# Moving the read-back of attention sums within the rounds of a macaron transformer block

## The chip, the cores and the metric

The kernel runs on one core of a Trainium2 chip. A core has five engines that run side by side: TensorE (matrix products, PE in the profile), VectorE (DVE), ScalarE (ACT), GpSimd (POOL) and SyncE (SP), which here does nothing but issue transfers (DMAs). Each engine works through its own instructions in order. The metric is the time of one launch on the device in microseconds (us); lower is better.

## The reference

One layer in the macaron form: half a feed-forward block, attention, half a feed-forward block, each on the layer-normed input and each added to it. The input is 2 sequences of 1024 tokens, 256 channels.

```python
x = x + 0.5 * ffn(layernorm(x))
x = x + attn(layernorm(x))      # q, k, v with bias, rotary turn, causal
x = x + 0.5 * ffn(layernorm(x))

# attn: 32 query heads of 8 channels, 8 key/value heads, each shared by 4 query heads
scores = einsum('bhqd,bhkd->bhqk', q, k_rep) / sqrt(8)
attn   = softmax(where(kpos > qpos, -inf, scores))
out    = einsum('bhqk,bhkd->bhqd', attn, v_rep)
return out.reshape(B, T, C) @ Wo + bo

# ffn: keep the 2 largest of each 4 hidden values
h = silu(x @ w_gate) * (x @ w_up)
return sparsify_2to4(h) @ w_down
```

## The kernel before

**Units and rounds.** Attention is cut into 16 units, one for each sequence `b` and key/value head `g`; a unit holds 4 query heads, taken as two pairs. Each unit has two passes. Pass 1 (`pass1`, L584 and the masks at L599) computes scores and takes their row maxima on VectorE (L613). Pass 2 (`pass2`, L669) computes the transposed scores with the maximum already subtracted, ScalarE takes the exponential (L679), and `weighted` (L706) multiplies by the values. A value tile has a column of ones beside the values, so the sum of the exponentials comes out of the same product.

Round `n` works on three units at once: pass 2 of unit n−1 (`prev`), pass 1 of unit n (`cur`), and the preparation of unit n+1 (`nxt`). The order of these pieces is written out by hand in the text `order`: `p1` and `p2` are pieces of the passes, `av k` multiplies piece `k` by the values, `neg1` and `shift` turn maxima into rows, and `prep` transposes the next unit (L529, `hT`), copies it (`stage`) and sends it to its place by 14 transfers (L543 zeros, L550 `kT`, L557 `qT`). The rounds from 1 on run under a hand-given schedule for TensorE and GpSimd; VectorE, ScalarE and SyncE are put in order by the scheduler of the language, which may place an instruction earlier or later than the text has it.

**Rows of maxima.** `shift` transposes the maxima (L640), copies them to `mrow` (L648), and sends four rows of 2x512 values, one for each head, into `qT` (L651). The first two heads (0 and 1) use strips of pair 0, the last two (2 and 3) those of pair 1. The rows of half 1 are first needed by `p2 3 1`, which is pass 2 on pair 1.

**PSUM.** Score tiles (`s`), the transposes `hT` and the output product share three buffers of two banks each, so TensorE is never more than three such tiles ahead of VectorE and ScalarE.

**From the products to the output.** When a unit has finished half of its queries (`av 2` for the first half, `av 9` for the second), `oT` is copied out of PSUM (L716) and stored to a buffer `avs` in DRAM (L717). After the last unit of a sequence, `output(b, blk)` brings the whole half together. It is a generator with stages: first it reads the sums and the products back from `avs`, eight transfers (L730 `sums`, L731 `heads`); then comes a reciprocal on VectorE (L733), its store to DRAM (L735 `recs`) and four transfers that spread it (L737 `heads<-recs`); then the multiplication (L742) and the product with `wo` (L753), which for the first sequence are made much later, in the last part of the attention. So for the first sequence the stages up to L737 happen inside the rounds of the second sequence:

- first half: `av 2` of round 8 makes the generator and takes its first stage at once; the second stage is called at `av 5` of round 9;
- second half: `av 9` is placed early in the order, and this one is made by round 9, which takes the first stage at once; the second stage is called at `av 5` of round 10.

The lists are `outs` (all generators), and `divisions` (those whose second stage is still to come).

Of the kernel before, what the change touches and what calls it, by code (L numbers as in the profile page):

```python
# [35 lines left out]
def macaron_kernel(  # L36
# [349 lines left out]
    def attention(actx, beside_first, beside_last, outs):  # L386
# [419 lines left out]
        units = [(b, g) for b in range(B) for g in range(NKV)]  # L806
        made = {}
        beside = []
        divisions = []

        def step(op, prev, cur, nxt):
            kind, *arg = op
            if kind == "p1" and cur is not None:
                cur.pass1(*steps1[arg[0]], arg[1:] or (0, 1))
            elif kind == "p2" and prev is not None:
                es = prev.pass2(*steps2[arg[0]], arg[1:] or (0, 1))
                made.setdefault(arg[0], (prev, {}))[1].update(es)
            elif kind == "av" and arg[0] in made:
                unit, es = made.pop(arg[0])
                qh, kbs = steps2[arg[0]]  # L820
                last = arg[0] in (2, 9)
                unit.weighted(qh, kbs, es, last)
                if last and unit.g == NKV - 1:
                    outs.append(output(unit.b, qh))
                    next(outs[-1])
                    if unit.b < B - 1:
                        divisions.append(outs[-1])
            elif kind == "neg1" and prev is not None:
                prev.negated(1)
            elif kind == "shift":  # L830
                unit = prev if arg[0] == 1 else cur
                if unit is not None:
                    unit.shift(arg[0])
            elif kind == "prep" and nxt is not None:
                nxt.prepare()
# [18 lines left out]
        def a_step():  # L854
            while beside and next(beside[0], beside) is beside:
                beside.pop(0)

        def round_(n, prev, cur):
            nxt = Unit(*units[n + 1]) if n + 1 < len(units) else None
            if n == 1:  # L860
                beside.append(second)
            if nxt is not None and nxt.b == 1:
                for _ in second:
                    pass
            firsts = 0
            for i, op in enumerate(ops):
                step(op, prev, cur, nxt)
                if i == first and cur is not None:
                    cur.negated(0)
                if n == 0 and i == first:  # L870

                    nc.scalar.activation(warm, cur.maxima[0][:, 0, 6:7], AF.Exp, scale=0.0)
                if n == 0 and op[0] == "p1":
                    firsts += 1
                    if firsts <= 12:
                        for _ in range(2 * (firsts % 2)):
                            next(beside_first, None)
                if n > 0:
                    for _ in range(2 if op in PAIRS else op[0] in ("av", "prep")):
                        a_step()  # L880
                if n > NKV and op == ("av", 5) and divisions:
                    next(divisions.pop(0))
            return cur, nxt

        engines = {mybir.EngineType.PE, mybir.EngineType.Pool}
        with tc.tile_pool(name="att_round0", bufs=2, side="right") as late["2"]:
            with tc.manual_schedule(engines=engines):
                prev, cur = round_(0, prev, cur)
                for _ in beside_first:
                    pass  # L890
# [6 lines left out]
        with tc.manual_schedule(engines=engines):  # L897
            for n in range(1, len(units)):
                prev, cur = round_(n, prev, cur)
        rctx.close()  # L900
        yield
        with tc.manual_schedule(engines=engines | {mybir.EngineType.DVE}):
            for op in parsed(last_order):
                if op[0] == "b":
                    next(beside_last, None)
                else:
                    step(op, prev, None, None)
            for _ in beside_last:
                pass

    with ExitStack() as fctx:
        actx = ExitStack()
        gens, outs = {}, []
# [23 lines left out]
        with last_units:  # L937
            first = FFN(0, False, f0 := ExitStack(), wd_sb, last_pool)
            att = attention(actx, first.down_slowly(NTB - 1), second_starts(), outs)
            with f0:  # L940
                first.run(
                    """
                    l0 l0 l0 l1 g0 l1 g0 l2 g0 g0 l2 g0 m l1 g0 g0 l2 m g0 m g1 m g1 m g1 m
                    g1 g1 m g1 d0 m a d0 l3 a p g1 p g1 m g2 m p g2 m g2 m p p p g2 p d1 m m
                    g2 m d1 a a l3 g2 p g2 l3 p g2 m p g3 p p m g3 p p m g3 g3 g3 m g3 m g3
                    m g3 p m m m d2 d2 a a
                    """,
                    {"p": att},
                )
            next(att)  # L950
# [71 lines left out]
```

## Time and profile before

| | us |
|---|---|
| median of 3 runs | 820.93 |
| lowest, highest | 820.42, 822.25 |
| profiled execution | 824.67 |
| its span, first to last instruction | 822.9 |
| TensorE busy | 786.1 |
| VectorE busy | 654.7 |
| ScalarE busy | 426.9 |
| GpSimd busy | 236.2 |

The profiled execution is one run of its own, with a time somewhat above the median. Its mean granted TensorE clock is 0.99 of full speed. Timelines give start and length of each instruction from the start of the span; an idle time before an instruction stands in brackets with what ended it. `SPq` is SyncE's queue: a line there is the issue of a transfer, not its landing. In shapes such as `64*128 64x512` the first is the stationary operand. A round lasts about 25.7 us when nothing disturbs it; round 10 begins at about 460 us of the span.

### The profile page before, as it was taken

The page shows a single profiled execution, that of the slowest core. Times are in us where ns is not written, and L with a number is a line of the kernel's source. Part 1 is how long each engine was busy: PE and PEld are TensorE (multiplying, and loading weights), DVE is VectorE, ACT ScalarE, POOL GpSimd, SP SyncE. Part 2 cuts the span into 40 slices and gives each one's busy share as a digit, 9 for nine tenths or more (in the row PEclk, how much of TensorE's full clock was granted, in tenths as well). Part 3 has the DMA queues.
Part 4 walks back from the last instruction along what each step waited for, and adds up shares of the span by engine and source line. Part 5 has one row for each costly group of instructions (what it writes and reads, how often), then busy time and mean ns, then how long its engine had stood idle before and what let it go on. Part 6 is the DMA issues. An engine that isn't in the chain of part 4 may idle for free.

```text
span 822.9 us, 13949 instructions
## 1 busy us (share of the span) xinstructions
PE 786.1 (96%) x5344; PEld 426.4 (52%) x5344; DVE 654.7 (80%) x871; ACT 426.9 (52%) x531; POOL 236.2 (29%) x443
## 2 busy tenths in 40 slices
PE   5999999998899999999999999999999999999998
PEld 2447574476544444454444444444445445657466
DVE  4797999898768796888888788888885479788692
ACT  1331313211677776877787687878877423122210
POOL 3000294821265465464222322233223100000000
PEclk9999999999999999999999899999999999999999
DMA  8100000022213222311333323322202200000001
GB/s 276 31 0 2 0 2 0 0 41 41 33 27 64 44 46 50 67 31 44 66 68 70 93 65 68 56 44 51 57 28 92 74 1 16 1 26 1 11 16 51
DMA packets 31010, 36.03 MB, mean 44 GB/s; under 512 B 12896, under 2 KB 20960, under 8 KB 30944
## 3 DMA queue, kind: packets, MB, share of 16 engines
q1 hardware_dynamic: 29118, 31.85, 17.2%
q10 hardware_dynamic: 1826, 3.29, 1.2%
q8 instruction: 42, 0.69, 0.4%
q14 instruction: 24, 0.20, 0.1%
HBM read 10.75 MB, written 10.75 MB: 26 GB/s over the span
## 4 chain that ended last, share of the span: by engine, by line
PE 71%; DVE 22%; ACT 4%; issue 1%; POOL 1%; DMA 0%; DVEq 0%; ACTq 0%
PE gu L252 20%; PE av L706 16%; PE s L584 9%; PE s L669 9%; PE o L307 9%; DVE maxima L613 8%; ACT e L679 3%; DVE h L292 2%; PE pr L474 2%; PE oo L753 2%; DVE h L262 1%; DVE sg L261 1%; DVE b L275 1%; PE s L599 1%; PE hT L529 1%
## 5 line engine op out<-in xcount | busy, mean ns | idle before, releaser
L613 DVE TENSOR_REDUCE maxima<-s 128x2 f32<-128x1024 f32 (+2 forms) x288 | 343.2, 1220 | 67.2 <-PE s L584 44.3
L679 ACT ACTIVATE e<-s 128x1024 f32<-128x1024 f32 x288 | 287.4, 1023 | 83.4 <-PE s L669 75.1
L706 PE MATMUL av<-e,vaug 128*32 128x512 f32 (+3 forms) x1536 | 158.5, 501 | 0.0
L685 POOL TENSOR_SCALAR_AFFINE_SELECT e<-e 128x256 f32<-128x256 f32 (+1 forms) x224 | 98.3, 451 | 201.5 <-ACT e L679 201.0
L584 PE MATMUL s<-kT,qT 64*128 64x512 f32 (+3 forms) x768 | 133.3, 386 | 14.6 <-ACT e L679 11.7
L669 PE MATMUL s<-qT,kT 64*128 64x512 f32 (+3 forms) x768 | 134.7, 395 | 3.1 <-DVE maxima L613 2.2
L252 PE MATMUL gu<-xnT,wg_sb 128*128 128x512 f32 x256 | 122.3, 600 | 0.7 <-ACT xnT L206 0.7
L252 PE MATMUL gu<-xnT,wu_sb 128*128 128x512 f32 x256 | 120.4, 593 | 0.0
L307 PE MATMUL o<-wd_sb,h 128*128 128x256 f32 x512 | 116.6, 386 | 0.9 <-DVE x L340 0.8
L584 PEld LDWEIGHTS s<-kT,qT 64*128 64x128 f32 x768 | 67.9, 187 | 82.7 <-ACT e L679 37.2
L307 PEld LDWEIGHTS o<-wd_sb,h 128*128 128x128 f32 x512 | 98.1, 193 | 18.5 <-issue 3.7
L669 PEld LDWEIGHTS s<-qT,kT 64*128 64x128 f32 x768 | 67.5, 186 | 62.1 <-DVE maxima L613 32.9
L260 ACT ACTIVATE sg<-gu 128x512 f32<-128x512 f32 x64 | 38.0, 593 | 113.6 <-PE gu L252 113.6
L263 ACT ACTIVATE a<-h 128x512 f32<-128x512 f32 x64 | 40.3, 630 | 104.9 <-DVE h L262 104.8
L252 PEld LDWEIGHTS gu<-xnT,wu_sb 128*128 128x128 f32 x256 | 48.9, 191 | 61.8 <-issue 61.8
L261 DVE TENSOR_TENSOR sg<-sg,gu 128x512 f32<-128x512 f32 x64 | 43.6, 681 | 46.1 <-ACT sg L260 46.0
L252 PEld LDWEIGHTS gu<-xnT,wg_sb 128*128 128x128 f32 x256 | 48.6, 192 | 54.6 <-issue 50.0
L181 POOL TENSOR_TENSOR rstd<-ve,neg_half 128x4 f32<-128x4 f32 x12 | 12.2, 1015 | 194.1 <-DVE ve L179 192.3
L706 PEld LDWEIGHTS av<-e,vaug 128*32 128x32 f32 x1536 | 34.1, 109 | 50.2 <-issue 38.8
L262 DVE TENSOR_TENSOR h<-sg,gu 128x512 f32<-128x512 f32 x64 | 43.9, 687 | 2.2
L599 PE MATMUL s<-half_id,half_mask 64*128 64x64 bf16 (+1 forms) x768 | 43.8, 205 | 0.0
L292 DVE SCALAR_TENSOR_TENSOR h<-w,h 128x512 f32<-128x512 bf16 x64 | 43.7, 743 | 0.0
(80 smaller groups left out, 562.4 us busy)
## 6 DMA issues: line engine op xcount, KB each, us to landing
avs<-oT SPq DMA_DIRECT2D x32, 256.0 KB
qT<-stage SPq DMA_DIRECT2D x124, 64.0 KB
kT<-stage SPq DMA_DIRECT2D x124, 32.0 KB
qT<-mrow SPq DMA_DIRECT2D x128, 4.0 KB
heads<-avs SPq DMA_DIRECT2D x16, 128.0 KB
out<-x SPq DMA_DIRECT2D x7, 256.0 KB
wu_sb<-in_wu SPq DMA_DIRECT2D x2, 512.0 KB
wg_sb<-in_wg ACTq DMA_DIRECT2D x2, 512.0 KB
```

Of the source, the lines that this page charges most:

```text
L252: nc.tensor.matmul(out=gu[:, i, :], lhsT=w_sb[:, kc, gb, j, :], rhs=self.xnT[tb][:, kc, :], start=(kc == 0), stop=(kc == 1),)
L261: nc.vector.tensor_tensor(sg, sg, gu[:, 0, :], ALU.mult)
L262: nc.vector.tensor_tensor(h[:, j, :], sg, gu[:, 1, :], ALU.mult)
L292: nc.vector.scalar_tensor_tensor(h[:, j, :], w[:, j, :], at, h[:, j, :], op, ALU.mult)
L307: nc.tensor.matmul(out=o[:, i, :], lhsT=self.hms[tb][k // 4][:, k % 4, bass.ts(2 * t2 + i, P)], rhs=self.wd_sb[:, k // 4, k % 4, :], start ...
L584: nc.tensor.matmul(out=to[:, i, s, bass.ds(col, n)], lhsT=self.qT[strip, pair, bass.ts(qt, P)].bitcast(FR), rhs=self.kT[strip, bass.ds(kc ...
L599: nc.tensor.matmul(out=last.rearrange("p (t n) -> p t n", n=P)[:, :, bass.ts(h, STRIP)], lhsT=half_mask[strip, h, :], rhs=half_id[strip, N ...
L613: ins = nc.vector.tensor_reduce(dst, src, AX.X, ALU.max, negate=True)
L669: nc.tensor.matmul(out=to[:, i, s, bass.ds(col, n)], lhsT=self.kT[strip, bass.ts(kb, P)].bitcast(FR), rhs=self.qT[strip, pair, bass.ds(q0, ...
L679: nc.scalar.activation(e, to, AF.Exp, scale=SCALE)
L685: nc.gpsimd.affine_select(out=first, in_=first, pattern=[[0, 2], [0, len(pairs)], [1, P]], compare_op=ALU.is_ge, fill=0.0, base=0, channel ...
L706: nc.tensor.matmul(out=self.av[32 * i : 32 * i + 32, TB - n : TB], lhsT=vaugs[self.b][:, kb, bass.ds(self.g * VW, 32)], rhs=es[i][:, bass. ...
```

## The change

The first stage of `output` (the eight read-backs of L730 and L731) is no longer taken at once for the first sequence. The generator goes on a list `stored`, and at `av 4` of the same round all of that list take their first stage and pass to `divisions`. For the first half this is `av 4` of round 8, for the second half `av 4` of round 9. For the second sequence nothing changes. The second stages are still called at `av 5` of rounds 9 and 10.

```diff
         beside = []
+        stored = []
         divisions = []
...
                 if last and unit.g == NKV - 1:
                     outs.append(output(unit.b, qh))
-                    next(outs[-1])
                     if unit.b < B - 1:
-                        divisions.append(outs[-1])
+                        stored.append(outs[-1])
+                    else:
+                        next(outs[-1])
...
                 if n > NKV and op == ("av", 5) and divisions:
                     next(divisions.pop(0))
+                if op == ("av", 4):
+                    for out_ in stored:
+                        next(out_)
+                    divisions.extend(stored)
+                    stored.clear()
```

In the built program the order on TensorE, ScalarE and GpSimd is the same as before. On SyncE and VectorE, around the end of round 9 and the start of round 10, it becomes (with the number of instructions; `mrow_1` are the rows of unit (1,1)):

```
SyncE before                          SyncE after
avs<-oT  (unit 7, second half)        avs<-oT  (unit 7, second half)
qT<-mrow_1 x3                         qT<-mrow_1 x4
sums, heads <-avs x8                  avs<-oT  (unit 8, first half)
qT<-mrow_1                            sums, heads <-avs x8
avs<-oT  (unit 8, first half)         recs<-sums (first half)
recs<-sums (first half)               qT<-mrow_1 x3      (next half)
qT<-zeros                             heads<-recs x4
heads<-recs x4                        qT<-mrow_1
qT<-mrow_1 x4      (next half)        qT<-zeros
kT, qT <-stage ...                    kT, qT <-stage ...

VectorE before                        VectorE after
maxima p1 1                           maxima p1 1
reciprocal (second half)              maxima p1 5 0
maxima p1 5 0                         maxima p1 0 0
maxima p1 0 0                         maxima p1 9 0
maxima p1 9 0                         reciprocal (second half)
maxima p1 0 1                         maxima p1 0 1
```

## Prediction

> **What bounds the kernel now.** I read the page first, then the timeline of the round in which the change acts, engine by engine, then busy time by stretch with the granted clock, and last the order of instructions on each engine in the two built programs.
>
> From the page, busy time and span:
>
> ```profile
> span 822.9 us, 13949 instructions
> PE 786.1 (96%) x5344; PEld 426.4 (52%) x5344; DVE 654.7 (80%) x871; ACT 426.9 (52%) x531; POOL 236.2 (29%) x443
> ```
>
> TensorE is occupied for 96% of the span, so only what leaves TensorE idle, or slows its clock, can cost or bring time. SyncE (the queue that issues nearly all DMAs) counts only where a matmul waits for a transfer.
>
> The change acts in rounds 8 to 10 of the attention, about 425 to 495 us. The timeline of SyncE's queue at the end of round 9 and the start of round 10:
>
> ```profile
> 451.58 0.51 SPq L717 DMA_DIRECT2D avs<-oT  x1
> 452.19 1.97 SPq L651 DMA_DIRECT2D qT<-mrow  x3
> 455.88 0.31 SPq L730 DMA_DIRECT2D sums<-avs  x1
> ...
> 459.57 0.59 SPq L651 DMA_DIRECT2D qT<-mrow  x1
> ...
> 460.69 0.41 SPq L735 DMA_DIRECT2D recs<-sums  x1
> ...
> 462.58 1.75 SPq L737 DMA_DIRECT2D heads<-recs  x4
> 464.42 2.48 SPq L651 DMA_DIRECT2D qT<-mrow  x4
> ```
>
> The read of the second half's sums stands behind its own store (451.58) and waits for it until 455.88; the fourth row of maxima for unit (1,1), ready long before, is queued behind it and leaves at 459.57. The waits of this queue put that wait at 1.6 us. Does TensorE pay for it? The timeline of TensorE where those rows are used, and the same place one round later:
>
> ```profile
> 460.74 0.50 PE L669 MATMUL s<-qT,kT 64*128 64x512 f32 x2
> 461.44 0.55 PE L669 MATMUL s<-qT,kT 64*128 64x512 f32 x2
> ...
> 464.94 0.93 PE L529 MATMUL hT<-ident_r,part 128*80 128x128 f32 x8 [0.80 <-DVE maxima L613]
> ...
> 493.45 0.79 PE L529 MATMUL hT<-ident_r,part 128*80 128x128 f32 x8 [0.20 <-DVE maxima L613]
> ...
> 497.83 0.50 PE L669 MATMUL s<-qT,kT 64*128 64x512 f32 x2
> ```
>
> The pair that needs the late row starts at 461.44, 0.70 after the pair before it. One round later the same two start at 489.86 and 490.56, also 0.70 apart. So the late row arrives just in time, and the wait that the change removes is worth nothing, 0.07 us at most (0.55 against 0.48 for the pair). The row at 464.94 shows what does cost: the transposes for the next unit wait 0.80 for VectorE instead of 0.20. VectorE's timeline says why:
>
> ```profile
> 461.72 1.23 DVE L613 TENSOR_REDUCE maxima<-s 128x4 f32<-128x1024 f32 x1 [0.27 <-PE s L599]
> 462.86 0.94 DVE L733 RECIPROCAL sums<-sums 128x128 f32<-128x128 f32 x1
> ```
>
> The reciprocal of the second half's sums stands in the row of maxima for which TensorE waits. And behind it, in the busy times by stretch (columns: stretch, its length, busy PE, PEld, DVE, ACT, POOL, granted clock, DMA share, GB/s):
>
> ```profile
> 305.00:308.42 3.42, 2.74 (x24) 1.36 (x22) 3.42 (x5) 2.23 (x3) 2.32 (x5) 1.00 0.51 78
> 308.42:311.83 3.41, 3.41 (x24) 1.41 (x26) 2.74 (x3) 2.45 (x3) 3.41 (x4) 0.50 0.52 82
> 441.54:444.95 3.41, 2.71 (x24) 0.90 (x16) 3.41 (x5) 2.67 (x3) 0.71 (x2) 1.00 0.47 71
> 462.02:465.43 3.41, 2.18 (x25) 1.61 (x25) 3.41 (x4) 2.81 (x4) 1.40 (x5) 1.00 0.31 86
> 465.43:468.84 3.41, 3.41 (x27) 1.86 (x25) 1.80 (x2) 2.43 (x3) 0.61 (x2) 0.50 0.11 20
> 468.84:472.26 3.42, 3.42 (x28) 1.35 (x24) 2.43 (x3) 1.16 (x2) 1.10 (x3) 0.50 0.53 78
> 464.94:493.45 28.51, 27.25 (x257) 13.17 (x257) 21.82 (x22) 20.39 (x23) 7.03 (x18) 0.88 0.30 64
> 493.45:519.10 25.65, 24.58 (x256) 12.11 (x256) 21.82 (x22) 20.73 (x24) 7.05 (x18) 1.00 0.27 56
> ```
>
> After a stretch with 1.23 us of TensorE idle (3.41 less 2.18) the clock is halved for 6.8 us, and the round from 464.94 lasts 28.51 instead of 25.65: 2.86 us lost. The same happened once before, at 308, after 0.68 idle. But 0.70 idle (441.54) did not do it.
>
> **The change, part by part.** In the built programs all engines but SyncE and VectorE keep their order.
>
> *First half (round 8).* Its eight transfers are called five steps later in the text but stand at the same place of SyncE's queue, and its reciprocal at the same place of VectorE's. Worth 0.
>
> *Second half, reads.* Eight transfers of about 0.46 each (455.88 to 459.47) go behind the fourth row of maxima and the next unit's store. They still start when their own store has landed, 455.88, and end at about 459.5, when the queue has nothing urgent: the next row is ready only at 463.9 (the copy at 463.32 lasts 0.57). The fourth row leaves 5 us earlier; by the 0.70 above, worth 0 to −0.07. I take 0.
>
> *Second half, reciprocal.* It moves three maxima later, behind that of p1 9 0. Before, it made the transposes late: 461.37 (exponential) to 464.94 is 3.57, one round later 490.48 to 493.45 is 2.97: it costs 0.60 there. In its new place VectorE has 0.25 of slack ahead of the next maximum (496.26 in the clean round), so 0.94 − 0.25 = 0.7 remain. The reciprocal of the first half, which stands two maxima further on in round 9, agrees: from the transposes to the products of av 1 (437.99 to 447.32) takes 9.33 against 8.62 in the clean round (493.45 to 502.07), 0.71.
>
> *Second half, what is pushed back in the queue.* recs<-sums of the first half (0.41) stays ahead of round 10's rows of maxima, in time when the queue is empty. But heads<-recs (four transfers, 1.75) now stand between the third and the fourth row, and qT<-zeros (0.68) behind the fourth. This adds a wait. Clean-round times less 29.11 (490.48 − 461.37) give round 10: rows start at 463.92, three take 1.97, heads<-recs 1.75 and 0.15 between, so the fourth starts at 467.8, not at 465.85. Its landing is shown by no row. Bounds: not before its issue ends (0.6, so no wait at all); recs<-sums needs 1.89 from issue to the transfer that waits for it (460.69 to 462.58), and the row issued at 459.57 was used at 461.44, 1.87. I take 1.9: landed at 469.7. The matmul that needs it (p2 3 1, second strip) would run at 497.83 − 29.11 = 468.72: 1.0 us late, between 0 and 1.0. Everything on TensorE queues behind it, and ScalarE's exponential (498.39) starts as its pair ends, so a delay here reaches the path whole. It runs beside the 0.7 of the reciprocal, for TensorE waits once for the later of the two: 1.0 together, 1.7 if they added.
> The transfers of the next unit start 2.2 us later (zeros 0.7, rows 1.5) and end at about 480.7 instead of 478.5; the rows of shift 0 behind them end at 484 instead of 481.8 and are first used at 489.86 (the place of 460.74 one round on). The cover is 5.9 us, the landing 1.9; nothing.
>
> *Sum for round 10:* −0.6 + 1.0 = +0.4 us (ends −0.6 and +1.1), without the clock.
>
> *The clock.* Here a rule and the trace disagree. The trace halves the clock after 1.23 us and after 0.68 us of idle in pieces within 3.41 us. The Trainium skill, "TensorE: Matmul & The Clock Gate", section "HAM oscillation — how this bites in real kernels", puts the abstract rule as no idle gaps over about 3.4 us. By the rule neither kernel loses clock here, and the sum is +0.4 whatever moves. By the row, the idle that leaves (0.6 at 464) was worth 2.86 us in this execution, and the idle that comes (up to 1.0 at 469) can cost as much. I follow the row.
> The sum against the profiled execution: 824.67 (span 822.9, 1.8 around it) + 0.4 is 825.1 with a half-speed stretch, and 822.2 without. It lies 3.7 above the median of 820.93. Taking off 2.86 and at most 1.7 (half of the 3.41 at 308) leaves 820.1, about the lowest run shown (820.42). So the runs behind the median mostly lack these stretches, and the change can't take from the median what is not in it: 820.93 + 0.4 = 821.3.
>
> **The rivals.** What a measurement of this kernel tells from no change is about 0.2%, 1.6 us.
> *A, forecast, 0.48: nothing to be seen.* 821.3, its own range 820.3 to 822.4. For it: the removed wait had no one waiting.
> *B, 0.34: slower.* The late fourth row and the reciprocal now fall within 2 us of each other, just ahead of 0.30 of idle that every round has (499.47 in the clean one). With 1.0 that is 1.3 us of idle within 3 us, as much as the 1.23 that halved the clock, and closer together, so that in most executions one stretch holds it. Price: one half-speed stretch 1.7, two 2.86, and 0.4: 823.0 to 824.2, say 823.5. It decides if idle in one stretch passes a point between 0.7 and 1.2. Against it: before had as much idle and its runs mostly show no loss.
> *C, 0.18: faster.* The runs of before do hold the half-speed stretch of round 10, the profiler's own cost hides it in my comparison, and moving the reciprocal ends it: 820.93 − 2.86 + 0.2 = 818.3. Against it: the lowest run would then have to hold it too.
> *That the change does not do what it says* holds for its first half, which does not move; it is part of A.
>
> **How the numbers follow.** Within 0.2% is 819.3 to 822.6. A gives 0.44 to no change, 0.03 to slower, 0.01 to faster; B 0.33 slower, 0.01 same; C 0.16 faster, 0.02 same. Faster 0.17, same 0.47, slower 0.36. The range from 818.4 to 823.7 takes in A, most of C and most of B; about 0.1 is left on each side.
>
> **What would show it.** In the profile after: the fourth row of maxima at about 454.2 and its pair still at 461.44; transposes of round 10 with 0.20 of idle; heads<-recs between the third and fourth row, and the first pair of p2 3 1 up to 1.0 late (right for the new wait; if it is on time, rows land faster than 1.9). Wrong would be A if most executions show the clock halved at 469 to 476 (B), or if the runs drop by over 1.6 us with no half-speed stretch in round 10 (C). A round 10 longer than 27 us at full clock would mean that the two delays add.

## The result, and the profile after

| us | before | changed |
|---|---|---|
| median of 16 runs each, same chip | 820.70 | 822.95 |
| lowest, highest | 820.09, 822.87 | 821.74, 826.08 |
| profiled execution (its span) | 824.67 (822.9) | 822.53 (820.8) |

The ratio is 1.0027, with a 95% interval of 1.0016 to 1.0038: slower by about a quarter of a per cent, 2.25 us between the medians. This ratio, here and below, compares all runs of both kernels; it is not the quotient of the medians, and since the times fall into several humps the two can differ. The two profiled executions stand the other way round, because that of before happened to hold a double half-speed stretch. So neither can be read without the granted clock.

The page of the changed kernel, span and busy times:

```profile
span 820.8 us, 13948 instructions
PE 782.9 (95%) x5344; PEld 425.6 (52%) x5344; DVE 655.2 (80%) x871; ACT 426.7 (52%) x531; POOL 236.2 (29%) x443
```

Nothing in these totals tells of a slower kernel. The timeline of SyncE's queue at the end of round 9 and the start of round 10 (start, length, issue):

```profile
450.85 2.63 SPq L651 DMA_DIRECT2D qT<-mrow  x4
...
458.03 0.37 SPq L735 DMA_DIRECT2D recs<-sums  x1
...
462.59 1.90 SPq L651 DMA_DIRECT2D qT<-mrow  x3
464.58 2.74 SPq L737 DMA_DIRECT2D heads<-recs  x4
467.36 0.59 SPq L651 DMA_DIRECT2D qT<-mrow  x1
467.99 0.67 SPq L543 DMA_DIRECT2D qT<-zeros  x1
```

The first line has all four rows of maxima together: the row that waited for a store now leaves at once. The cost stands lower down: `heads<-recs` lies between the third row and the fourth, and takes 2.74, where it took 1.75 before. TensorE in the same stretch:

```profile
459.41 0.50 PE L669 MATMUL s<-qT,kT 64*128 64x512 f32 x2
460.11 0.48 PE L669 MATMUL s<-qT,kT 64*128 64x512 f32 x2
...
463.01 0.79 PE L529 MATMUL hT<-ident_r,part 128*80 128x128 f32 x8 [0.21 <-DVE maxima L613]
...
467.56 0.50 PE L669 MATMUL s<-qT,kT 64*128 64x512 f32 x1
...
469.09 0.50 PE L669 MATMUL s<-qT,kT 64*128 64x512 f32 x1 [1.02 <-DMA qT<-mrow]
...
491.33 0.79 PE L529 MATMUL hT<-ident_r,part 128*80 128x128 f32 x8 [0.20 <-DVE maxima L613]
```

The pairs at 459.41 and 460.11 are 0.70 apart, just as before: the early row brought nothing. The transposes at 463.01 wait 0.21 and no longer 0.80. Then the two strips of `p2 3 1`, which belong together, come 1.53 apart: the second waits 1.02 for the fourth row. The kernel before has them together at this place (from another execution of it, of 820.03 us):

```profile
467.58 0.50 PE L669 MATMUL s<-qT,kT 64*128 64x512 f32 x2
...
469.23 0.50 PE L584 MATMUL s<-kT,qT 64*128 64x512 f32 x2 [0.30 <-ACT e L679]
```

VectorE in the changed kernel:

```profile
464.35 1.23 DVE L613 TENSOR_REDUCE maxima<-s 128x2 f32<-128x1024 f32 x1 [0.26 <-PE s L599]
465.49 0.94 DVE L733 RECIPROCAL sums<-sums 128x128 f32<-128x128 f32 x1
466.35 2.29 DVE L613 TENSOR_REDUCE maxima<-s 128x8 f32<-128x1024 f32 x2
```

The reciprocal now stands behind the transposes and just ahead of the late row. Busy times by stretch: rounds 9 and 10, from transposes to transposes, and then two stretches inside round 10 (stretch, length, busy PE, PEld, DVE, ACT, POOL, granted clock, DMA share, GB/s):

```profile
436.64:463.01 26.37, 24.63 (x257) 12.07 (x257) 22.54 (x23) 20.72 (x24) 7.05 (x18) 1.00 0.37 83
463.01:491.33 28.32, 25.99 (x256) 13.15 (x256) 22.73 (x23) 20.92 (x24) 7.06 (x18) 0.94 0.32 72
467.61:471.02 3.41, 1.90 (x12) 1.08 (x12) 2.19 (x3) 1.40 (x2) 0.38 (x1) 1.00 0.27 57
471.02:474.43 3.41, 3.41 (x28) 2.14 (x30) 2.63 (x4) 2.55 (x4) 0.45 (x2) 0.50 0.50 78
```

A stretch in which TensorE was idle for 1.5 (3.41 less 1.90: the 1.02 for the late row, and 0.49 behind it, where a round without the late row has 0.30) is followed by 3.41 at half clock. Round 10 becomes 28.32.

What before costs undisturbed is seen in the execution of 820.03 us. Its rounds 9 and 10:

```profile
436.26:463.21 26.95, 24.61 (x256) 12.11 (x256) 23.25 (x24) 21.22 (x24) 7.11 (x19) 1.00 0.39 90
463.21:488.87 25.66, 24.57 (x257) 12.07 (x257) 21.83 (x22) 20.23 (x23) 7.07 (x18) 1.00 0.32 70
```

The two rounds take 52.61 here and 54.69 in the changed kernel, 2.08 more. The loss of this execution lies in them: from the end of round 10 to the end of the span it is 329.43 here (818.3 − 488.87) and 329.47 in the changed kernel (820.8 − 491.33). The 2.25 between the medians is of the same size, but the medians mix executions with different clocks.

### The profile page after: what moved, and what is told of

Its sections match the earlier page's. It is cut to its first block, busy times and chain, and to the rows that moved or that the text cites. A ratio compares the mean times of both kernels' runs of the same rounds, so it can differ in the third digit from the quotient of the medians.

```text
span 820.8 us, 13948 instructions
## 1 busy us (share of the span) xinstructions
PE 782.9 (95%) x5344; PEld 425.6 (52%) x5344; DVE 655.2 (80%) x871; ACT 426.7 (52%) x531; POOL 236.2 (29%) x443
## 4 chain that ended last, share of the span: by engine, by line
PE 71%; DVE 23%; ACT 4%; issue 1%; DMA 1%; POOL 0%; DVEq 0%; ACTq 0%
PE gu L252 20%; PE av L706 15%; PE s L584 9%; PE s L669 9%; DVE maxima L613 9%; PE o L307 9%; ACT e L679 3%; DVE h L292 2%; PE pr L474 2%; PE oo L753 2%; DVE h L262 1%; DVE sg L261 1%; DVE b L275 1%; PE hT L529 1%; PE s L599 1%
## 5 line engine op out<-in xcount | busy, mean ns | idle before, releaser
L706 PE MATMUL av<-e,vaug 128*32 128x512 f32 (+3 forms) x1536 | 156.7, 496 | 0.0
```

The costliest lines, as they stand in the source:

```text
L706: nc.tensor.matmul(out=self.av[32 * i : 32 * i + 32, TB - n : TB], lhsT=vaugs[self.b][:, kb, bass.ds(self.g * VW, 32)], rhs=es[i][:, bass. ...
```

## Experiments

Theory: the late fourth row, with what it does to the clock, makes the change slower. Rivals: the moved reciprocal does, or the read-backs behind their store. Kernels of one group ran on one chip, each group with its own runs of before.

### Group 1: take the two parts apart (before: 820.97, 67 runs)

**The transfers ahead of the rows.** The changed kernel, with `heads<-recs` of the first half issued ahead of all four rows, so that the fourth is no longer held up. They are put in a function that `shift` calls, and pinned in the queue:

```diff
-            for j in range(4):
-                nc.sync.dma_start(out=heads[...], in_=rec...)
+            def spread():
+                for j in range(4):
+                    ins = nc.sync.dma_start(out=heads[...], in_=rec...)
+                return ins.ins
+            if (b, blk) == (0, 0):
+                late["spread"] = spread
+            else:
+                spread()
...
-                for h in range(REP):
+                for h in range(REP + 1):
+                    now = half == 1 and h == 0 and "spread" in late
+                    ...   held = late["spread"](), rows pinned behind it
```

> The changed kernel, with one thing put back: the four transfers heads<-recs of the first half go ahead of all four rows of maxima of round 10, in the 4 us in which SyncE's queue is empty, instead of between the third and the fourth row. The moved reads and the moved reciprocal stay. Theory (the late fourth row is the cause): no wait for a row at p2 3 1 (1.02 us of idle in the changed kernel, 0 here), round 10 from transposes to transposes about 26.4 us at full clock, median 820.6 to 821.1, as before. Rival 1 (the reciprocal in its new place is the cause, 0.7 us and the idle that halves the clock): stays at 822.5 to 823. Rival 2 (the moved reads disturb other transfers): stays at 822.5 to 823.

Measured: 820.47 (22 runs), ratio 0.9988 [0.9977, 0.9999], slightly faster than before. SyncE, TensorE and the rounds:

```profile
460.67 1.74 SPq L751 DMA_DIRECT2D heads<-recs  x4
462.51 2.48 SPq L664 DMA_DIRECT2D qT<-mrow  x4
```

```profile
467.38 0.50 PE L682 MATMUL s<-qT,kT 64*128 64x512 f32 x2
```

```profile
436.45:462.82 26.37, 24.61 (x256) 12.11 (x256) 22.53 (x23) 20.72 (x24) 7.10 (x18) 1.00 0.39 91
462.82:488.82 26.00, 24.71 (x256) 12.08 (x256) 22.52 (x23) 20.83 (x24) 7.09 (x18) 1.00 0.33 71
```

Both strips run together ("x2") with no wait, the clock stays whole, and round 10 is 26.00. The reciprocal stands where the change put it, so its own price there is 26.00 − 25.66 = 0.34. The loss of the change went with the order of four transfers and one row; the read-backs stand behind their store here too, so that rival falls. (The scheduler also put `qT<-zeros` ahead of the rows here; the run with the transfers last, below, has it behind them, and loses nothing either.)

**The same order, put into before.** Before, with `heads<-recs` between the third and the fourth row of round 10 (the `now` above at `h == 3`). The reciprocal stays ahead of the transposes, where before has it; the scheduler also put `qT<-zeros` ahead of the rows.

> The kernel before, with one thing of the change alone: heads<-recs of the first half go between the third and the fourth row of round 10. Reads and reciprocal stay where they were. Theory: the fourth row lands about 1.5 us too late, TensorE waits at p2 3 1, and with the 0.6 us of the reciprocal ahead of the transposes the idle adds up: 822.2 to 824, slower by 1.5 to 3. Rivals 1 and 2: nothing of what they blame is changed here, 820.7.

Measured: 824.66 (22 runs), ratio 1.0024 [1.0012, 1.0036]. The median is above what I expected; how much of it is the stretch that before itself can have behind its late transposes was not separated. TensorE at the row, and round 10:

```profile
469.04 0.50 PE L682 MATMUL s<-qT,kT 64*128 64x512 f32 x1 [0.91 <-DMA qT<-mrow]
```

```profile
463.27:491.32 28.05, 25.98 (x256) 13.27 (x256) 22.01 (x22) 20.43 (x23) 7.09 (x18) 0.94 0.32 71
```

Before becomes slow by this order alone, with nearly the same idle (0.91 against 1.02) at the same instruction, and the same halved clock.

**The reciprocal alone.** Before, with only the reciprocal of the second half moved to where the change has it:

```diff
+            pin = {1: (1, 2, "71", (0,))}      # the maximum of p1 9 0 in round 10
+            with ExitStack() as order:
+                if b == 0 and blk in pin:
+                    order.enter_context(tc.issue_after(late[pin[blk]]))
                 nc.vector.reciprocal(sums, sums)
```

> The kernel before, with the reciprocal of the second half alone moved three maxima later, to its place in the changed kernel. Transfers stay. Theory: 0.6 us leave at the transposes and 0.7 come later, 820.6 to 821.0, no difference. Rival 1 (the reciprocal's new place is the cause): 822 to 823.

Measured: 821.60 (14 runs), ratio 0.9995 [0.9980, 1.0010], no difference. Its rounds 9 and 10:

```profile
436.58:462.95 26.37, 24.90 (x256) 12.26 (x257) 22.54 (x23) 20.69 (x24) 7.06 (x18) 1.00 0.39 88
462.95:488.98 26.03, 24.73 (x257) 12.10 (x257) 22.53 (x23) 20.83 (x24) 7.05 (x18) 1.00 0.34 74
```

Round 9 gains 0.58 and round 10 gives back 0.37. The median lies between what the theory and the rival expected (820.6 to 821.0, 822 to 823), so it decides little by itself. But the interval ends at 1.0010, none of the 14 runs has a mean clock under 0.994, and with the transfers first the reciprocal stood at this same place and nothing was lost. So the rival falls: the reciprocal alone doesn't make the loss.

**Both mended.** The changed kernel with the transfers first, and each of the two reciprocals pinned behind the latest maximum at `av 5`, where VectorE has slack.

> The changed kernel with heads<-recs ahead of the rows, and both reciprocals of the first sequence moved into the second part of their rounds, where VectorE idles 0.4 to 0.9 us ahead of each maximum. If both reciprocals cost 0.6 and 0.7 where they stood before, this gains 1.3 us on the kernel before and loses the idle that halved the clock in round 10: 819.0 to 819.6. If a reciprocal is hidden wherever it stands, 820.7.

Measured: 820.12 (22 runs), ratio 0.9982 [0.9971, 0.9992]. This version is faster than before here, and its median lies below that of the changed kernel in all three comparisons (822.40 at the least). That it beats the one with the transfers first is not shown: the intervals overlap.

```profile
436.30:462.15 25.85, 24.77 (x256) 12.03 (x256) 22.62 (x23) 20.73 (x24) 7.05 (x18) 1.00 0.42 94
462.15:488.01 25.86, 24.78 (x256) 12.07 (x256) 22.62 (x23) 20.73 (x24) 7.05 (x18) 1.00 0.32 70
```

Together 51.71 against 52.61, so 0.90 is gained in these rounds, and the median gains 0.85. That is less than I had expected: the rounds stay 0.2 above the 25.66 of a round with no reciprocal in the way. TensorE is busy for 0.2 longer in them (24.77 against 24.57); why was not tested.

### Group 2: dose, place, and what is left (before: 820.77, 51 runs)

**The changed kernel once more**, as the measure for this group.

> The changed kernel itself, once more, so that the three below stand beside it on one chip: 822 to 823.5, slower than before by about 2.2. Of these, by the first profile, 1.3 are the wait at p2 3 1 and what it drags along, about 1.0 the half-speed stretch behind it where it comes, 0.6 a saving at the transposes and 0.35 the reciprocal in its new place. If so, runs without a half-speed stretch are about 1.2 to 1.6 above the lowest runs of before, and the rest of the scatter goes with the clock.

Measured: 822.40 (22 runs), ratio 1.0021 [1.0011, 1.0031]. This execution is one in which the late row does not halve the clock:

```profile
465.46 2.28 SPq L737 DMA_DIRECT2D heads<-recs  x4
```

```profile
469.50 0.50 PE L669 MATMUL s<-qT,kT 64*128 64x512 f32 x1 [0.57 <-DMA qT<-mrow]
```

```profile
463.88:490.74 26.86, 24.94 (x256) 12.42 (x256) 22.53 (x23) 20.71 (x24) 7.09 (x18) 1.00 0.34 76
```

The four transfers took 2.28 here, the row made TensorE wait 0.57, and the round is 26.86: its time without the clock. With 26.39 in round 9 (437.49 to 463.88) the two take 53.25, 0.64 above before.

**Twice the transfers.** The changed kernel, with the four transfers made twice ahead of the fourth row (`late["spread"]()` called two times at `h == 3`).

> The changed kernel with the four transfers heads<-recs issued twice between the third and the fourth row (the second time over the same data), eight instead of four. Theory: the fourth row leaves 1.8 us later and TensorE waits 1.8 us longer, about 2.8 instead of 1.0; median 1.8 above the changed kernel or more, since a longer idle halves the clock more surely: 824.5 to 826. Rival (the wait is made up later in the round, or the clock alone decides): no more than 0.5 above the changed kernel.

Measured: 825.80 (6 runs), ratio 1.0058 [1.0043, 1.0073].

```profile
471.33 0.49 PE L682 MATMUL s<-qT,kT 64*128 64x512 f32 x1 [2.91 <-DMA qT<-mrow]
```

```profile
463.38:495.09 31.71, 27.47 (x256) 13.52 (x256) 22.71 (x23) 20.95 (x24) 7.09 (x18) 0.89 0.32 72
```

Against this group's own execution of the changed kernel, the transfers take 2.32 longer (4.60 for eight, 2.28 for four), and the wait grows by 2.34, from 0.57 to 2.91. Round 10 now holds 6.83 at half speed (a mean clock of 0.89), where that execution had none and the first profile 3.41. The median grows by 3.4. The effect follows the dose.

**The transfers last.** The changed kernel, with `heads<-recs` behind the fourth row (`h == 4`).

> The changed kernel with heads<-recs behind the fourth row. The fourth row is then on time (issued at about 464.5 of the changed kernel's time), and what is pushed back is the zeros and the next unit, by nothing against the changed kernel. Theory: as good as putting them ahead of the rows, 820.2 to 821.0. Rival (any transfer beside the rows slows their landing): between this and 822.9.

Measured: 820.14 (14 runs), ratio 0.9987 [0.9976, 0.9999]. SyncE and round 10:

```profile
463.34 2.56 SPq L664 DMA_DIRECT2D qT<-mrow  x4
465.99 2.22 SPq L751 DMA_DIRECT2D heads<-recs  x4
```

```profile
463.75:489.76 26.01, 24.72 (x256) 12.08 (x256) 22.52 (x23) 20.85 (x24) 7.08 (x18) 1.00 0.35 78
```

The same round as with the transfers first. It is only the place between two rows that costs; pushed behind them, they hold nothing up that matters.

**The reciprocal into slack, the row left late.** The changed kernel, with only the second half's reciprocal pinned behind the latest maximum at `av 5`. By a rival, the reciprocal's idle beside that of the row is what tips the clock.

> The changed kernel, the late fourth row included, with the reciprocal of the second half alone moved into the idle time of VectorE later in round 10. Theory (wait and reciprocal run side by side, and the row is the later): nothing changes in the wait, at most 0.35 less, 822.2 to 823.2, still slower than before by 1.5 or more. Rival (it takes both together to cost, by adding up or by halving the clock): back to 821.3 or below.

Measured: 822.74 (22 runs), ratio 1.0018 [1.0008, 1.0028], no better than the changed kernel beside it.

```profile
470.11 0.50 PE L670 MATMUL s<-qT,kT 64*128 64x512 f32 x1 [0.73 <-DMA qT<-mrow]
```

```profile
464.50:492.83 28.33, 26.37 (x257) 12.92 (x257) 22.81 (x23) 20.94 (x24) 7.08 (x18) 0.94 0.32 72
```

The clock is halved all the same, so the late row does it without the reciprocal beside it.

Why here, with a wait of 0.73, and not in the changed kernel beside it, with 0.57? The traces have more to say than the size of the wait. Within one execution, the half-speed stretches start a whole number of 3.413 us apart (in before at 202.60, 308.42 and 465.43, which is 31 and 46 such steps; in the changed kernel at 204.78 and 471.02, 78 steps), and between executions these steps lie differently against the work. Counted on from the one half-speed stretch of the changed kernel's execution (203.75), and from that of this run (472.54):

```profile
466.58:469.99 3.41, 2.72 (x29) 1.26 (x25) 3.00 (x4) 1.56 (x3) 1.44 (x3) 1.00 0.26 74
469.99:473.41 3.42, 2.91 (x33) 1.72 (x28) 2.91 (x3) 3.12 (x4) 0.46 (x2) 1.00 0.45 68
```

```profile
469.13:472.54 3.41, 2.19 (x18) 1.25 (x17) 2.02 (x4) 1.90 (x2) 0.55 (x2) 1.00 0.30 50
472.54:475.95 3.41, 3.41 (x26) 1.72 (x28) 2.81 (x3) 2.58 (x4) 0.24 (x1) 0.50 0.51 81
```

The idle time is the same, 1.20 and 1.22 in all, but the first execution has it divided over two steps (0.69 and 0.51), and the second has all of it in one. The kernel before shows the same: its idle time at the late transposes and just ahead of them fell into two steps (0.52 and 0.80) in the undisturbed execution, and into one (1.23) in its first profile. In the fourteen traces, between 215 and 600 us, all six steps with 1.22 or more of idle are followed by half speed, one of six with 0.95 to 1.15, and one with 0.68. No run moved the steps on purpose.

### Groups 3 and 4: fill the idle time (before: 820.71, 25 runs, and 821.15, 35 runs)

If it is idle time that halves the clock, matmuls without use in that time should keep the clock whole while the row stays late. The changed kernel, with ten matmuls ahead of `p2 3 1`, whose results the real ones overwrite:

```diff
+                if (self.b, self.g, qh, kbs[0], tuple(pairs)) == (1, 1, 1, 0, (1,)):
+                    for k in range(2 * 5):
+                        nc.tensor.matmul(out=to[:, k % 2, 0, :], lhsT=self.kT[...], rhs=self.kT[...],
+                                         start=True, stop=True)
```

> The changed kernel, its late fourth row and its reciprocal untouched, with ten matmuls (five on each strip, 64x512) put on TensorE ahead of p2 3 1 of round 10. They write the score tile that p2 3 1 overwrites, so they leave the result as it is and only keep TensorE at work for about 1.2 us of its wait. Theory (about half of the loss is the half-speed stretch that the idle brings): the row is as late as before, but idle ahead of it is 0.4 or less, the clock stays whole in round 10, round 10 lasts 26.7 to 27.0, and the median is 0.7 to 1.2 below the changed kernel: 821.2 to 821.8. Rival (the wait alone is the whole loss, the clock scatters by itself): no gain, 822.4 to 823.

Measured: 822.62 (21 runs), ratio 1.0014 [1.0004, 1.0024]. The fill (the line without `qT`), the transfers, and round 10:

```profile
466.85 1.42 PE L667 MATMUL s<-kT 64*128 64x512 f32 x10
468.12 0.74 PE L679 MATMUL s<-qT,kT 64*128 64x512 f32 x2
```

```profile
463.87 2.72 SPq L747 DMA_DIRECT2D heads<-recs  x4
```

```profile
462.29:489.60 27.31, 25.99 (x266) 13.31 (x266) 22.54 (x23) 20.72 (x24) 7.08 (x18) 1.00 0.34 75
```

The row is as late as in the first profile (2.72 for the transfers), but the clock stays at 1.00 and round 10 is 27.31, about 1.0 below 28.32. This one execution does not show that the fill did it: a step of 3.41 ends at 467.93 in it (from the stretch at 201.67), amid the idle that is filled, so that the clock might have stayed whole without it. The median does not follow: 822.62 misses what I expected, and 7 of the 21 executions had a mean clock of 0.993 or less.

One more execution of before in the same group gave the undisturbed rounds shown at the top.

> The kernel before, one more look, for the length of rounds 9 and 10 in an execution in which the clock may stay whole: if it does, 26.95 and 25.6 to 25.9 from transposes to transposes, against 26.37 and 26.0 with the reciprocal moved. If the clock is halved again in round 10, 28.5 as in the first profile.

Then more of the same: fourteen matmuls there, and four more ahead of the pair before.

> As the run with ten extra matmuls, with fourteen ahead of p2 3 1 and four ahead of p2 3 0, so that the second gap of the changed kernel (0.49 us ahead of p1 9 1) is made smaller too. The row stays late. Theory (the idle, not the lateness, brings the half-speed stretch): round 10 of 26.9 to 27.4 with the clock whole, some executions with a granted clock of 0.998 again (none of 38 of the changed kernel, 40 of 143 of the kernel before), and a median 0.5 to 1.0 below the changed kernel beside it. Rival (the clock scatters by itself): medians within 0.3 of each other and no execution at 0.998.

Measured: 821.81 (14 runs), ratio 1.0007 [0.9995, 1.0019].

```profile
462.64:490.15 27.51, 26.46 (x274) 13.68 (x275) 22.59 (x23) 20.97 (x24) 7.06 (x18) 1.00 0.34 75
```

The changed kernel beside it, on the same chip:

> The changed kernel beside the one with extra matmuls, on the same chip: 822.4 to 823, no execution with a granted clock of 0.998.

Measured: 822.40 (22 runs), ratio 1.0005 [0.9993, 1.0016].

```profile
462.36:490.68 28.32, 25.98 (x256) 13.10 (x257) 22.73 (x23) 20.94 (x24) 7.06 (x18) 0.94 0.32 72
```

These two executions can be compared: their steps lie alike against round 10 (one starts 4.63 behind the transposes with the fill, 4.61 without). In that step the kernel without the fill has 1.50 of idle (466.97 to 470.38) and then half speed; the one with it has 0.06, and its clock stays whole:

```profile
467.27:470.68 3.41, 3.35 (x30) 2.32 (x30) 2.08 (x3) 1.20 (x2) 0.34 (x1) 1.00 0.29 61
```

So in this pair the idle time, and not the lateness, halved the clock, and the round is 27.51 against 28.32. The median is 0.6 lower, but the intervals overlap, and no execution reached a clock of 0.998, though I had expected that of some. What share of the median is the clock's is not settled by these two. And on this chip the change itself shows no sure loss. Over the three comparisons the ratio of the changed kernel was 1.0027, 1.0021 and 1.0005.

### How often the clock was halved

Each execution has its mean granted clock. One stretch of 3.41 at half speed takes 3.41 × 0.5 / 820, or 0.002, from it.

| executions | number | clock 0.998 or more | 0.993 or less |
|---|---|---|---|
| before (groups 1 to 4) | 178 | 46 | 25 |
| changed (first result, groups 2 and 4) | 60 | 0 | 21 |
| changed, transfers first | 22 | 7 | 0 |
| changed, transfers last | 14 | 6 | 0 |
| before, reciprocal alone | 14 | 4 | 0 |
| both mended | 22 | 7 | 0 |
| before, transfers between the rows | 22 | 0 | 13 |
| changed, reciprocal into slack | 22 | 0 | 4 |

No execution of a kernel with the transfers between two rows and no fill has the best clock; of the other kernels in the table, a quarter or more do. With the fill it was 4 of 21 and 0 of 14. This shows, in the runs behind the medians and not in one profile alone, that the late row costs clock in at least a part of them. The part can't be counted: the mean clock does not say in which round a stretch fell, and 27 of the 60 executions of the changed kernel have 0.996, which a profile with a halved round 10 has (before with the transfers between the rows) and one without (group 2).

The last column holds something else. All 25 executions of before in it have 0.990, the clock of the first profile with its double stretch behind the late transposes, and a median of 824.83. None of the 72 executions with the reciprocal moved and the row on time is in it. So it looks as if the change also took away a loss that before has in about one execution of seven, and the late row hid that gain; only the one profile shows in which round it lies.

## Where the prediction was right and where it was wrong, point by point

The forecast was 821.3, nothing to be seen, and the result is 822.95, slower. It lies inside the range only because the range was drawn wide enough to take in most of rival B; it lies outside forecast A's own range (up to 822.4) and just under B's 823.0 to 824.2.

**Right.** *The removed wait had no one waiting*: the fourth row leaves early and its pair still comes 0.70 after the one before. *The reciprocal leaves the place ahead of the transposes, −0.60*: 26.95 − 26.37 = 0.58. *The new wait*: `heads<-recs` between the third and the fourth row, and the second strip of `p2 3 1` waiting for it; this carries the result. *The transfers of the next unit cost nothing when later*: with the transfers last or first, round 10 shows no other wait.

**Mis-sized, the reciprocal in its new place.** Taken as 0.7 from the first half's place in round 9; it is 0.34 (26.00 − 25.66).

**Mis-sized, the issue of four `heads<-recs`.** Taken as 1.75 from the row of before. Behind the rows they took 2.22 to 2.86. So the second strip, which stands 4.56 behind the transposes when the row is in time (467.38 − 462.82), stood 6.08 behind them in the first profile (469.09 − 463.01) and 5.62 in the whole-clock execution (469.50 − 463.88): 1.5 and 1.06 late, where I had bounded it at 1.0.

**Half right, "1.0 together, 1.7 if they added".** With the row 1.06 late and the reciprocal worth 0.34, round 10 grew by 26.86 − 25.66 = 1.20, between the larger alone (1.06) and their sum (1.40). Net of round 9 it is +0.64 where I had +0.4. This part of the sum was about right; the medians could not have told +0.4 from nothing, with intervals of about 0.1% (0.8) to each side.

**The step that failed: "the change can't take from the median what is not in it".** I had argued that the runs of before mostly lack half-speed stretches, and so forecast none for the changed kernel. But that before seldom loses clock says nothing of a kernel with a new idle piece of 1.0. What the runs showed in its place is rival B's mechanism: the late row falls beside the idle that every round has there (B had 0.30; it became 0.49), and together, 1.5 in one step of 3.41, they halve the clock. The reciprocal, which B counted in, is not needed for it (0.73 and 0.49 were enough with it moved away). B's price came out near, in part by luck: 3.41 at half speed cost 0.8 to 1.0 (28.32 against 27.51 and 27.31 with the fill) where I had put 1.7 (half of 3.41), but the row was later than I had put it, and together it came to 2.08. B's "point between 0.7 and 1.2" is not a sharp one: 1.22 or more in one step always halved the clock, 0.95 to 1.15 once in six, and my own rows had 0.68 that did and 0.70 that did not. And it holds for the idle within one step. That answers what I set against B, that before had as much idle and mostly no loss: in its undisturbed execution this idle was divided over two steps.

**Rival C had a part of the truth.** Before can hold the half-speed stretch of round 10, by the mean clock in about one execution of seven (25 of 178), so the median would show next to nothing of its end.

**Rule against row.** The Trainium skill ("TensorE: Matmul & The Clock Gate", "HAM oscillation — how this bites in real kernels") asks only that idle gaps stay under about 3.4. Here 1.5 within a stretch of 3.41, in pieces of at most 1.02, halved the clock, so the measurement decides. To follow the row was right; I followed it for the price and then did not carry it into the forecast.

**The comparison of profiled times.** I held 824.67 for the clock's bad luck and worked from the median. That was right: before undisturbed gave 820.03.

## What to carry to other kernels

When an edit frees a queue early, list what the moved instructions now stand in front of: here eight transfers left a place where nobody waited, and four others came to stand ahead of one row that TensorE needs at once. A delay of one microsecond on an engine that is otherwise full has two prices, itself and the clock that the idle time may cost; ask of each new wait what other idle time lies within a few microseconds of it. Mending the order of four transfers, and placing the two small VectorE instructions in slack, gave a version faster than before (0.9982 [0.9971, 0.9992]).

## What was not expected of the hardware

- The clock can be halved after short idle pieces: 3.41 us at half speed followed a stretch with 1.5 idle, and 6.83 us one with 2.31, from a wait of 2.91. The price is not the length: the 3.41 cost 0.8 to 1.0, the 6.83 in the profile of before 55.46 − 52.61 = 2.85 (its rounds 9 and 10 against undisturbed ones).
- Whether a given wait halves the clock differs between executions of one kernel: the changed kernel's round 10 was 28.32, 26.86 and 28.32 in three profiles. In the traces it went with where the idle falls against steps of 3.41, which lie differently in each execution. The times come in humps (before: 46 executions at a clock of 0.998 with a median of 820.35, 25 at 0.990 with 824.83), and the same comparison on three occasions gave 1.0005 to 1.0027.
- Four `heads<-recs` take 1.73 to 1.75 to issue from an idle queue, and 2.22 to 2.86 right behind three or four rows of maxima: 2.22 to 2.28 in the three profiles of group 2, 2.71 to 2.86 in the five others. Each group ran on its own chip, so this may be the chip's; why was not found.
